# First edge layer of a two-layer graph network: GpSimd's half rows of messages in quarters, gathers in four parts

## The chip, the core and the metric

The kernel is written in Bass and Tile for one core of a Trainium2 chip. The metric is the device time of one execution in microseconds. TensorE is called PE in the profile, VectorE DVE, ScalarE ACT, GpSimd POOL, and SyncE, which issues most plain DMAs, SP. Each engine takes its own instructions in the order of the program; an instruction that has to wait for another engine, or for a DMA, holds up all that stands behind it on its engine.

## What is computed

A graph with 6,250 nodes of 512 features and 100,000 edges, sorted by their destination, goes through two layers with a layernorm and a ReLU ahead of each and a residual around each. The change is in the first one, an attention layer with 8 heads of 64 features:

```python
h = leaky_relu(feat @ W.T + b, 0.2).reshape(N, 8, 64)
e = leaky_relu(e_src[src] + e_dst[dst], 0.2)      # one logit per edge and head
m = segment_max(e, dst); ex = exp(e - m[dst]); s = segment_sum(ex, dst)
a = ex / s[dst] * dist
msg = h[src] * a[:, :, None]                      # a row of 512 per edge, scaled head by head
out = segment_sum(msg, dst)
```

The second layer takes the mean of `x[src]` over each node's edges, two products with 512 x 512 weights, and a layernorm.

## The kernel before

**Tiles and windows.** The edges are cut into four streams (`q` = 0 to 3), each stream into tiles of 128 edges. A window `k` holds three tiles (`j` = 0, 1, 2) of every stream, so 12 tiles of 128 edges; there are 66 windows. Tile (q, j) is written with two digits here, as the program does: 32 is stream 3, third tile. The streams form two pairs, `p` = 0 (streams 0 and 1) and `p` = 1 (streams 2 and 3).

**Gathers.** GpSimd fetches each tile with one indirect DMA (line 744): 128 rows of `h0_d`, 520 fp32 each (512 features and 8 source logits), chosen by the edges' source indices, into `gbuf`. This buffer has room for four windows (`NB = 4`), so the gathers that are issued in window k are those of window k + 4, and each of them overwrites a tile of window k. Before it may be issued, the matmul that reads that tile has to be done.

**Messages.** A gathered row becomes a message when each of its heads is multiplied by that edge's weight (`weigh`, line 897). VectorE does whole pairs of tiles (`message`, line 967, 128x1024, for j = 0 and 1) and the first half row of tile 02 (`message_part`, line 974). The rest of the four tiles with j = 2 is shared: ScalarE does heads one by one (`message_act`, line 986), and GpSimd does the second half, heads 4 to 7, of tile 12 and of tile 32 (`message_pool`, line 998, 128x256). These two half rows are the steps `K0` (tile 12) and `K1` (tile 32).

**Sums.** `add_up(k, p, j)` (line 1010) adds a pair's messages into the destinations' rows: two matmuls with one-hot weights, 128x64 by 128x512 fp32, the first for stream 2p, the second for 2p + 1. The steps are `A00`, `A01`, `A02` for p = 0 and `A10`, `A11`, `A12` for p = 1. The second matmul of `A02` reads tile 12, that of `A12` tile 32; so `A02` needs `K0` and `A12` needs `K1`. `finish` (lines 1027 and 1028; `C0`, `C1`) adds what the window before carries over.

**Softmax ahead.** The logits of later windows are worked on at the same time: `front_turn` and `front_copy` (transposes of the one-hot tiles, lines 806 and 810; `FT0`, `FT1`), `front_dst` (line 818; `FD`, window k + 3), `soft_src` (line 827; `SSa`, `SSb`), scans on VectorE (lines 847, 854, 861), `soft_turn` (line 873; `TE`, `TM`), `soft_back` (line 878; `CM`), `leaky` to `weigh`. `add_ones` (line 1018; `SV`) sums the softmax weights.

**The order.** Nothing is scheduled by a compiler: the list `ORDER` (line 1172) is run through once for each window and writes every engine's instructions in that order. For PE it says, from one `A12` to the next: `A12 FD SSa C1`, then in the next window `TE FT1 A00 SV A01 TM A10 A02 SSb C0 A11 FT0 A12`. For GpSimd it says `K0`, then `GA`, six gathers, then `K1`, then `GB`, six gathers. `TILES` (line 1120) gives the gathers' order: `10 01 00 30 11 20` in `GA`, and `02 22 12 21 31 32` in `GB`. What each waits for follows from the tile that it overwrites: 10 and 00 wait for `A00`; 01 and 11 for `A01`; 30 and 20 for `A10`; 02 and 12 for `A02`; 21 and 31 for `A11`; 22 and 32 for `A12`.

A gathered tile is read first by `soft_pick` (line 835): tiles with j = 0 and 1 near the end of window k + 1, tiles with j = 2 early in window k + 2.

Of the kernel before, what the change touches and what calls it, by code (L numbers as in the profile page):

```python
# [12 lines left out]
OP = mybir.AluOpType  # L13
AX = mybir.AxisListType

N, D, E, H = 6250, 512, 100000, 8
# [6 lines left out]
T = 3  # L23
# [3 lines left out]
NB = 4  # L27
# [17 lines left out]
def gnn_kernel(ctx, tc, x, srcp, dstp, attrp, wt0, b0, wsrc, wdst, wts, wtn, bias1, gamma1, beta1, out):  # L45
    nc = tc.nc
    V, A, G, S, P = nc.vector, nc.scalar, nc.gpsimd, nc.sync, nc.tensor
# [629 lines left out]
    for t in range(NT):  # L677
        if t + 3 < NT:
            norm(t + 3)
            g, i = where[t + 3]  # L680
# [42 lines left out]
    GT, ES_, OHs, OHTs, PEN, AT, ZP, E_, PB, ET, MF, MR, NX, EX, AA, WS, WC, CS, FP, FD, RS, F9, SA, AP_ = ({} for _ in range(24))  # L723
    breg = {}

    def njof(k):
        return T if k < NW - 1 else 1
# [8 lines left out]
    def gather(k, part=None):  # L736
        GT[k] = g_ = gbuf[:, k % NB]
        tiles = [(q, j) for q, j in TILES if j < njof(k)]
        if k >= NW - 3:
            tiles.sort(key=lambda t: t[1])  # L740
        n = len(tiles) // 2
        for q, j in tiles if part is None else (tiles[:n], tiles[n:])[part]:
            c = k * T + j
            G.indirect_dma_start(out=g_[:, q, j, :], out_offset=None, in_=h0_d,  # L744
                                 in_offset=bass.IndirectOffsetOnAxis(ap=idx[:, q, c:c + 1], axis=0))
# [211 lines left out]
    BK, SV, A2 = {}, {}, {}  # L957
# [33 lines left out]

        return p == 0 and first <= k < NW and k % GRP[0] and k % GRP[1]

    def message_pool(k, p):

        if njof(k) == T and not (p and k in IDLE):
            x3 = GT[k][:, 2 * p + 1, T - 1, D // 2:D].rearrange("p (h d) -> p h d", d=D // H)
            G.tensor_tensor(out=x3, in0=x3, in1=A2[k][:, T - 1, 2 * p + 1, H // 2:H].unsqueeze(2).to_broadcast([128, H // 2, D // H]),  # L998
                            op=OP.mult)

    def add_up(k, p, j):
        if j >= njof(k):
# [114 lines left out]


    TILES = [(int(t[0]), int(t[1])) for t in """
    10 01 00 30 11 20 02 22 12 21 31 32  # L1120
    """.split()]

    for q in range(NQ):
# [1 line left out]
    for k in range(NB - 1):  # L1125
        gather(k)
# [5 lines left out]
    def later(f, end=NW):  # L1132

        return lambda k, *a: f(k, *a) if 0 < k < end else None
# [18 lines left out]
    def ahead(k, part):  # L1153
        if k >= NB - 1:
            gather(k, part)
# [3 lines left out]
        FT0=(4, front_turn, 0), FT0c=(4, front_copy, 0), FT1=(3, front_turn, 1), FT1c=(3, front_copy, 1),  # L1159
        FD=(3, front_dst), ECa=(3, soft_pick, 0), SSa=(3, soft_src, 0), ECb=(2, soft_pick, 1), SSb=(2, soft_src, 1), EZ=(2, soft_copy), SCF=(2, max_before), NX=(2, max_ahead),  # L1160
        SCR=(1, max_all), TE=(1, soft_turn, 0), TM=(1, soft_turn, 1), CM=(1, soft_back), LM=(1, leaky),
        SUB=(1, soft_sub), EXP=(1, soft_exp), AA=(1, weigh),
        FL=(1, later(fac_leaky, KR)), FDf=(1, later(fac_sub, KR)), FX=(1, later(fac_exp, KR)), RS=(1, later(fac_rows, KR)),
        RH=(1, later(fac_diag, KR)), PF=(1, later(fac_spread, KR)), F9a=(1, later(fac_rest, KR)), F9b=(1, later(fac_all, KR)),
        RESC=(0, later(rescale, KR)), D0c=(0, message_part), D0a=(0, message, 0, 0), D0b=(0, message, 0, 1), D1a=(0, message, 1, 0),
        D1b=(0, message, 1, 1),
        SV=(0, add_ones), A00=(0, add_up, 0, 0), A01=(0, add_up, 0, 1), A02=(0, add_up, 0, 2),
        A10=(0, add_up, 1, 0), A11=(0, add_up, 1, 1), A12=(0, add_up, 1, 2), C0=(0, finish, 0), C1=(0, finish, 1),
        EV0=(0, evac0), EV1=(-1, evac1), OH=(4, onehot), CS=(0, later(carry_sel)),
        GA=(NB, ahead, 0), GB=(NB, ahead, 1), K0=(0, message_pool, 0), K1=(0, message_pool, 1))  # L1170
    STEPS.update({f"H{p}{i}": (0, message_act, p, i) for p in range(2) for i in range(4) if p or i})
    ORDER = """
    K0 H01 D0b S D0a D1a TE ECb H11 NX S SCR S FT1 A00 D0c FL EV1 SV S H12 RESC A01 AT0 H02 OH TM A10 GA K1 S CM FDf
    A02 FX S RS S LM RH AT0c CS SSb C0 SUB PF L FT1c S EZ EXP D1b SCF S A11 H10 AT1 ECa AT1c FT0 S AA F9a S A12 F9b S
    EV0 FD SSa C1 FT0c S GB
    """.split()

    def late_x(i):
# [384 lines left out]
    def early(w, f):  # L1563
# [3 lines left out]

    STEPS1 = dict(EV0=(0, evac1_, 0), CS0=(-1, carry_split, 0), EV1=(-1, evac1_, 1), CS1=(-1, carry_split, 1), OH=(1, onehot, 3),
                  SEL=(1, carry_sel, FR), C0=(0, finish1, 0), C1=(0, finish1, 1), G0=(3, gather1, 0), G1=(2, gather1, 1))
    STEPS1.update({f"A{p}{j}": (0, add_up1, p, j) for p in range(2) for j in range(T)})  # L1570
    SLOTS1 = dict(MEAN=(-2, slot1_mean), SUMS=(-1, slot1_sums))
    ORDER1 = """
    en en la MEAN A00 A01 A02 la A10 CS0 C0 EV1 OH en PUT en PRE G1 sl la SEL en en SUMS CS1 sl A11 A12 EV0 G0 C1 sl
    """.split()

    last, ends = none(), none()
    for k in range(-1, NW - 1):
# [5 lines left out]
        for name in ORDER1:  # L1583
# [11 lines left out]
            elif name in SLOTS1:  # L1595
                d, f = SLOTS1[name]
# [7 lines left out]
    k = NW - 1  # L1604
# [53 lines left out]
    with tc.If(fv > 0):  # L1658
# [69 lines left out]
        with tc.For_i(0, NE * 128, 128) as r:  # L1728
# [12 lines left out]
                            in0=hg[:, 0:D].rearrange("p (h d) -> p h d", h=H),  # L1741
                            in1=ga.unsqueeze(2).to_broadcast([128, H, D // H]), op=OP.mult)
# [52 lines left out]
```

## Time and profile before

| what | us |
|---|---|
| median of three runs (2717.96, 2723.20, 2725.59) | 2723.2 |
| the profiled execution, its own time | 2745.03 |
| its span, first to last instruction | 2743.2 |
| from the span's start to the first edge layer, about | 265 |
| the first edge layer, about 265 to 1455 | 1190 |
| the second layer and what follows, about | 1288 |
| GpSimd busy over the span | 1795.8 |
| PE busy over the span (weight loads apart) | 2125.4 |

A group of instructions is shown as line, engine, operation, output and inputs, shape and count, then the busy time and the mean of one in ns, then the time that the engine sat idle just before them, and what ended most of it. In the timeline each row has start, duration, engine, line and count (xN), and in brackets the idle time before it and what ended it. A releaser named "issue" means that the profile shows nothing that was waited for; ends of matmuls are modelled.

### The profile page before, as it was taken

How to read it: one execution, taken by the hardware profiler on the slowest of the kernel's cores; microseconds unless marked ns; L12 is line 12 of the kernel's file. 1: busy time of each engine (PE TensorE's matmuls, PEld its weight loads, DVE VectorE, ACT ScalarE, POOL GpSimd, SP SyncE). 2: the span in 40 equal slices, each digit the busy share in tenths (PEclk: the TensorE clock that was granted, in tenths of full speed). 3: DMA queues.
4: the chain of work that ended last, by engine and by line, in shares of the span. 5: the costliest groups of instructions: out<-in, count | busy, mean ns of one | idle time of the engine just before them, and what ended most of it. 6: DMA issues, size and time to landing. Idle time of an engine off the chain costs nothing.

```text
span 2743.2 us, 32878 instructions
## 1 busy us (share of the span) xinstructions
PE 2125.4 (77%) x8780; PEld 1052.9 (38%) x8780; DVE 1539.0 (56%) x3120; ACT 984.8 (36%) x2957; POOL 1795.8 (65%) x1803
## 2 busy tenths in 40 slices
PE   7982688888888888888884376687878788787876
PEld 5761233333333333333331133343344334343434
DVE  7874565567666766665676222354445345454545
ACT  6860344444454454444453011122222122222212
POOL 4666477777777677767762666666667666666652
PEclk9996799999999899999997588898889889898988
DMA  6636477787878878878775777777878787787872
GB/s 203 208 114 182 129 206 198 222 246 233 241 229 243 243 237 237 247 228 235 237 232 152 231 213 220 242 252 248 251 248 264 240 255 238 248 256 246 253 221 88
DMA packets 264702, 611.54 MB, mean 223 GB/s; under 512 B 63604, under 2 KB 74372, under 8 KB 264510
## 3 DMA queue, kind: packets, MB, share of 16 engines
q0 software_dynamic: 125440, 414.35, 51.7%
q1 hardware_dynamic: 138494, 193.97, 21.6%
q8 instruction: 72, 1.18, 0.2%
q10 hardware_dynamic: 576, 1.05, 0.1%
q14 instruction: 120, 0.98, 0.1%
HBM read 511.44 MB, written 97.76 MB: 222 GB/s over the span
## 4 chain that ended last, share of the span: by engine, by line
PE 31%; issue 9%; DVE 7%; another core or an unknown queue 7%; DMA 2%; ACT 1%; POOL 1%; SPq 1%; ACTq 0%; DVEq 0%; POOLq 0%
PE ps_f L592 6%; PE ps_w L1325 5%; PE ps_s L1325 5%; PE ps_b L592 5%; PE ps_w L1010 3%; PE ps_w L1333 2%; DVE gbuf L967 1%; PE ps_z L818 1%; PE ps_t L1406 1%; PE ps_w L1027 1%; PE ps_z L1406 1%; PE ps_s L1333 1%; DVE sx L1090 1%; DVE oh L787 1%
## 5 line engine op out<-in xcount | busy, mean ns | idle before, releaser
L1296 POOL DMA_INDIRECT g<-h_d,idx x784 | 774.1, 987 | 386.5 <-issue 202.5
L744 POOL DMA_INDIRECT gbuf<-h_d,idx x784 | 770.5, 983 | 348.7 <-issue 179.4
L1010 PE MATMUL ps_w<-gbuf,oh 128*64 128x512 f32 x1568 | 517.2, 663 | 94.9 <-issue 52.9
L986 ACT ACTIVATE gbuf<-gbuf,aa 128x64 f32<-128x64 f32 x1276 | 329.8, 334 | 2.3 <-DVE aa L907 0.7
L967 DVE TENSOR_TENSOR gbuf<-gbuf,ps_c 128x1024 f32<-128x1024 f32 x260 | 308.0, 1212 | 0.3 <-issue 0.3
L1325 PE MATMUL ps_s<-g,oh 128*64 128x512 f32 x784 | 193.5, 629 | 51.9 <-issue 49.2
L1325 PE MATMUL ps_w<-g,oh 128*64 128x512 f32 x784 | 217.0, 636 | 12.6 <-issue 10.6
L1010 PEld LDWEIGHTS ps_w<-gbuf,oh 128*64 128x64 f32 x1568 | 103.8, 142 | 226.7 <-issue 156.5
L1423 ACT ACTIVATE hs<-sx,slc 128x512 f32<-128x512 f32 x45 | 36.6, 813 | 419.5 <-remote 186.4
L854 DVE TENSOR_TENSOR_SCAN nx<-penb,ms,ps_z 32x256 f32<-32x256 f32 x66 | 48.1, 729 | 223.2 <-PE ps_w L1010 90.7
L1412 DVE TENSOR_TENSOR lo<-ps_t,hi 128x512 fp32r<-128x512 f32 x55 | 37.9, 688 | 229.7 <-ACT hi L1411 105.6
L628 POOL TENSOR_TENSOR pr<-hr,watt 128x1024 f32<-128x1024 f32 x47 | 113.2, 2417 | 75.5 <-DVE hr L625 70.2
L810 ACT ACTIVATE oht<-ps_t 128x384 f32<-128x384 f32 x132 | 63.7, 482 | 233.0 <-PE ps_z L818 74.3
L592 PE MATMUL ps_f<-ws_whi,hi 128*128 128x512 f32 x112 | 58.1, 519 | 106.3 <-issue 61.5
L787 DVE TENSOR_TENSOR oh<-ps_c,dsr 128x768 f32<-128x768 f32 x130 | 123.0, 947 | 1.8 <-issue 1.8
L1038 ACT ACTIVATE ws<-ps_w 128x512 f32<-128x512 f32 x103 | 60.2, 584 | 172.7 <-PE ps_w L1010 86.4
L1027 PE MATMUL ps_w<-ws,cs 128*128 128x512 f32 x170 | 99.1, 666 | 20.8 <-DVE et L885 11.3
L818 PE MATMUL ps_z<-oht,edb 128*32 128x384 f32 (+1 forms) x264 | 112.9, 557 | 1.7 <-DVE mf L847 1.7
L1325 PEld LDWEIGHTS ps_s<-g,oh 128*64 128x64 f32 x784 | 52.5, 142 | 156.8 <-issue 143.4
L806 PE MATMUL ps_t<-ident,oh 128*128 128x128 f32 x392 | 79.1, 315 | 35.8 <-issue 31.0
L998 POOL TENSOR_TENSOR gbuf<-gbuf,aa 128x256 f32<-128x256 f32 x128 | 81.3, 636 | 38.0 <-issue 18.6
L1333 PE MATMUL ps_w<-chi,cs 128*128 128x512 f32 x65 | 36.2, 557 | 80.5 <-issue 47.8
(398 smaller groups left out, 4007.5 us busy)
## 6 DMA issues: line engine op xcount, KB each, us to landing
sx<-x SPq DMA_DIRECT2D x95, 256.0 KB
acc_d<-ws SPq DMA_DIRECT2D x182, 130.2 KB
acc_d<-ws SPq DMA_DIRECT2D x182, 128.0 KB
h_d<-hr SPq DMA_DIRECT2D x49, 260.0 KB
gbuf<-h_d,idx POOLq DMA_INDIRECT x784
g<-h_d,idx POOLq DMA_INDIRECT x784
sa<-acc_d SPq DMA_DIRECT2D x48, 260.5 KB
s<-acc_d SPq DMA_DIRECT2D x48, 256.0 KB
```

Of the source, the lines that this page charges most:

```text
L592: P.matmul(pt, a_[:, k], w_[:, k], start=not last[0], stop=stop and k == 3 and w_ is whi_ and a_ is lo)
L628: G.tensor_tensor(out=pr, in0=hr[:, None, 0:D].to_broadcast([128, 2, D]), in1=watt, op=OP.mult)
L744: G.indirect_dma_start(out=g_[:, q, j, :], out_offset=None, in_=h0_d, in_offset=bass.IndirectOffsetOnAxis(ap=idx[:, q, c:c + 1], axis=0))
L787: V.tensor_tensor(out=oh.rearrange("p a j b n -> p (a j b) n"), in0=c_iota[:, None, :].to_broadcast([128, 4 * T, M]), in1=dsr[:, k].rearra ...
L818: P.matmul(z[0:NQ * H, 0:n], ed_tile(k, p), oht[:, p, 0:n], start=(p == 0), stop=False, skip_group_check=True)
L967: eng.tensor_tensor(out=x4, in0=x4, in1=(AA if eng is V else A2)[k][:, i, q].unsqueeze(3).to_broadcast([128, 2, H, D // H]), op=OP.mult)
L986: A.activation(x_, x_, AF.Copy, scale=A2[k][:, T - 1, 2 * p + q2, h:h + 1])
L1010: P.matmul(w[r, :], oh[:, p, j, q2], g_[:, 2 * p + q2, j, 0:D], start=(j == 0 and not goes_on(k, p)), stop=False, skip_group_check=True)
L1027: P.matmul(w, CS[k][:, p], c[:, p, 0:D], start=False, stop=True, skip_group_check=True)
L1296: G.indirect_dma_start(out=g_[:, q2, j, :], out_offset=None, in_=h1_d[0:NT * 128, :], in_offset=bass.IndirectOffsetOnAxis(ap=idx[:, 2 * p ...
L1325: P.matmul(BK[p][64 * q2:64 * q2 + 64, :], OHs[k][:, p, j, q2], GT[k, p][:, q2, j, :], start=(j == 0 and not goes_on(k, p, 1)), stop=False ...
L1333: P.matmul(w, CS[k][:, p], part, start=False, stop=True, skip_group_check=True)
```

## The change

The second half of a row, heads 4 to 7, is now multiplied in two instructions of two heads each, 128x128 instead of 128x256. `K0` becomes `K00` (heads 4 and 5 of tile 12) and `K01` (heads 6 and 7); `K1` becomes `K10` and `K11` for tile 32. The twelve gathers are issued in four parts of three, `G0` to `G3`, and one quarter row stands ahead of each: `K00 G0 K01 G1 K10 G2 K11 G3`. In the list of tiles, 22 moves from the eighth place to the eleventh, so the parts are `10 01 00`, `30 11 20`, `02 12 21` and `31 22 32`. The steps of the other engines keep their order.

```diff
-        n = len(tiles) // 2
-        for q, j in tiles if part is None else (tiles[:n], tiles[n:])[part]:
+        n = len(tiles) // 4
+        for q, j in tiles if part is None else tiles[n * part:n * part + n]:
...
-    def message_pool(k, p):
+    def message_pool(k, p, i):
 
         if njof(k) == T and not (p and k in IDLE):
-            x3 = GT[k][:, 2 * p + 1, T - 1, D // 2:D].rearrange("p (h d) -> p h d", d=D // H)
-            G.tensor_tensor(out=x3, in0=x3, in1=A2[k][:, T - 1, 2 * p + 1, H // 2:H].unsqueeze(2).to_broadcast([128, H // 2, D // H]),
-                            op=OP.mult)
+            h = slice(H // 2 + 2 * i, H // 2 + 2 * i + 2)
+            x3 = GT[k][:, 2 * p + 1, T - 1, h.start * 64:h.stop * 64].rearrange("p (h d) -> p h d", d=D // H)
+            G.tensor_tensor(out=x3, in0=x3, in1=A2[k][:, T - 1, 2 * p + 1, h].unsqueeze(2).to_broadcast([128, 2, D // H]), op=OP.mult)
...
-    10 01 00 30 11 20 02 22 12 21 31 32
+    10 01 00 30 11 20 02 12 21 31 22 32
...
-        EV0=(0, evac0), EV1=(-1, evac1), OH=(4, onehot), CS=(0, later(carry_sel)),
-        GA=(NB, ahead, 0), GB=(NB, ahead, 1), K0=(0, message_pool, 0), K1=(0, message_pool, 1))
+        EV0=(0, evac0), EV1=(-1, evac1), OH=(4, onehot), CS=(0, later(carry_sel)))
+    STEPS.update({f"G{i}": (NB, ahead, i) for i in range(4)})
+    STEPS.update({f"K{p}{i}": (0, message_pool, p, i) for p in range(2) for i in range(2)})
...
-    K0 H01 D0b S D0a D1a TE ECb H11 NX S SCR S FT1 A00 D0c FL EV1 SV S H12 RESC A01 AT0 H02 OH TM A10 GA K1 S CM FDf
-    A02 FX S RS S LM RH AT0c CS SSb C0 SUB PF L FT1c S EZ EXP D1b SCF S A11 H10 AT1 ECa AT1c FT0 S AA F9a S A12 F9b S
-    EV0 FD SSa C1 FT0c S GB
+    K00 H01 D0b S D0a D1a TE ECb H11 NX S SCR S FT1 A00 D0c FL EV1 SV S H12 RESC A01 AT0 H02 OH TM A10 G0 K01 G1 K10 S
+    CM FDf A02 FX S RS S LM RH AT0c CS SSb C0 SUB PF L FT1c S EZ EXP D1b SCF S A11 G2 K11 H10 AT1 ECa AT1c FT0 S AA F9a
+    S A12 F9b S EV0 FD SSa C1 FT0c S G3
```

## The prediction

> **What bounds the kernel now.** I read the page's groups, then the sums by stage, then the waits of the gathers' line, then the timelines of GpSimd and PE for a window. The chain of waits gives little here: it follows PE and VectorE through this stage and hardly meets GpSimd.
>
> ```profile
> L744 POOL DMA_INDIRECT gbuf<-h_d,idx x784 | 770.5, 983 | 348.7 <-issue 179.4
> L998 POOL TENSOR_TENSOR gbuf<-gbuf,aa 128x256 f32<-128x256 f32 x128 | 81.3, 636 | 38.0 <-issue 18.6
> 265.00:1455.00 1190.00, 994.35 (x4248) 422.70 (x4250) 786.87 (x1516) 564.32 (x2102) 823.04 (x881) 0.91 0.77 225
>   issue: 179.4, 630
>   PE ps_w L1010: 49.6, 40
>   PE ps_z L818: 35.5, 23
>   PE ps_z L827: 28.1, 25
>   PE ps_s L1018: 12.4, 9
> ```
>
> The stage takes 1190 us, in which GpSimd is busy for 823 and PE for 994. A gather takes 0.95 us and the next starts 0.30 us later (the "issue" row, 179.4 us in 630 gaps), so it costs 1.25 us; twelve are 15.0 us. A half row is 0.62 us, followed by a gap of 0.16 in place of 0.30, so it adds 0.5; two add 1.0. Over the whole stage, the idle rows named PE sum to about 126 us in 97 waits: one and a half waits in each window, of 1.3 us. GpSimd's timeline shows where they sit: ahead of 22, of 10, or of 01.
>
> ```profile
> 1029.29 0.62 POOL L998 TENSOR_TENSOR gbuf<-gbuf,aa 128x256 f32<-128x256 f32 x1
> 1030.07 0.99 POOL L744 DMA_INDIRECT gbuf<-h_d,idx  x1 [0.16 <-issue]
> 1032.62 0.94 POOL L744 DMA_INDIRECT gbuf<-h_d,idx  x1 [1.57 <-PE ps_z L818]
> ...
> 1038.26 0.95 POOL L744 DMA_INDIRECT gbuf<-h_d,idx  x1 [0.30 <-issue]
> 1039.22 0.62 POOL L998 TENSOR_TENSOR gbuf<-gbuf,aa 128x256 f32<-128x256 f32 x1
> 1040.00 0.99 POOL L744 DMA_INDIRECT gbuf<-h_d,idx  x1 [0.16 <-PE ps_w L1010]
> ```
>
> ```profile
> 1029.96 1.07 PE L1010 MATMUL ps_w<-gbuf,oh 128*64 128x512 f32 x2 [2.31 <-issue]
> 1030.96 1.48 PE L818 MATMUL ps_z<-oht,edb 128*32 128x384 f32 x4
> ...
> 1034.77 1.08 PE L1010 MATMUL ps_w<-gbuf,oh 128*64 128x512 f32 x4
> 1035.78 1.51 PE L1018 MATMUL ps_s<-ex,oh 128*128 128x18 f32 x12
> 1037.22 1.08 PE L1010 MATMUL ps_w<-gbuf,oh 128*64 128x512 f32 x4
> ```
>
> K1 ends at 1029.91 and PE, idle for 2.31 us, starts the second matmul of `A12` at 1029.96. So **K1 gates A12**, and in most windows it does. Then PE runs without a gap through FD, SSa, C1, TE, FT1 to `A00` (ends 1034.77 + 1.08 = 1035.85, 5.94 after K1) and SV to `A01` (ends 1038.30, 8.39 after K1). This closes a ring: K1, A12, A00, gather 10, five more gathers, K1. GpSimd's own way round it is longer now: from K1's end it has six gathers and K0 to do, and reaches 10 after 8.2 us at the earliest (7.41 to K0 where nothing waits, 0.62, 0.16). Sixty ends of K1 between 315.91 and 1398.95 make 59 windows of **18.36 us**, 16.0 us of work, about 1.9 of waits for PE and 0.45 of gathers that take over 0.95.
>
> How late PE's word can be is shown by the waits themselves:
>
> ```profile
> 747.70 0.98 POOL L744 DMA_INDIRECT gbuf<-h_d,idx  x1 [1.78 <-PE ps_s L1018]
> 1096.50 0.94 POOL L744 DMA_INDIRECT gbuf<-h_d,idx  x1 [1.24 <-PE ps_z L827]
> ```
>
> The first is gather 10, 9.83 us after the end of K1 (737.87); the second is 01, 11.64 after it (1084.86), though the records draw `A01` as over by 1093.27. Such waits are seldom between 0.3 and 1 us: GpSimd goes on about 1.1 us or more after its last gather ended, even where the matmul is drawn as done before that. So I treat PE's drawn ends as a floor, not as the moment of release.
>
> **The change, part by part.**
>
> *Quarter rows.* Two 128x256 go, four 128x128 come, 4 a window for 62 windows. No 128x128 multiply of GpSimd is in this trace. Its rows of 128x256 (0.62 to 0.64 us) and 128x512 (1.23 to 1.28) give 2.4 ns an element with next to nothing fixed: 0.31. The nearest smaller one, 128x195 on line 382, takes 0.54. I take 0.33, nearer to the proportional end as the operation is the same. Each then adds 0.33 + 0.02 + 0.16 - 0.30 = 0.21, four 0.84, against 1.0 now: -0.2 us a window, +0.7 at the other bound. [...]
>
> *K11's place, the part that decides.* A12 now needs K11, which stands behind nine gathers, with three behind it. From its end GpSimd does 31, 22, 32 (0.16 + 0.99 + 0.30 + 0.95 + 0.30 + 0.95 = 3.65 us) and K00 (0.35), and stands at 10 after 4.2 us, or 5.4 where 22 waits as it does now. PE needs 5.94 at least for `A00` and 8.39 for `A01`. So gathers 10 and 01 wait in every window, and K01, G1, K10, G2 and K11 stand behind 01. That queue from the start of 01 to the end of K11:
> - 01 and 00: 0.95 + 0.30 + 0.95 = 2.20
> - K01: 0.02 + 0.33, then a gap of 0.16: 0.51
> - G1: 0.99 + 0.30 + 0.95 + 0.30 + 0.95 = 3.49; K10 0.51; G2 3.49; K11 0.35
>
> in all 10.55, and 0.30 more since a gather's mean is 983 ns and not 946 (8 x 37). The window is then the start of 01 after K11, plus 10.85. The start of 01 has three prices: 8.39 + 0.30 = 8.7 (drawn end, no delay); 11.7 (the usual start of 01 where it waits today, as 11.64 above); and what I take, **9.6**: GpSimd is at rest after 10, and its release comes some 1.1 us after that rest began, or 0.9 after `A01`. I lean to the low side since GpSimd now rests for 4 to 5 us a window just there. That makes 20.45.
>
> *K01's place.* `A02` needs K01, which now stands behind G0; it ends at 9.6 + 2.55 = 12.2 after K11, while PE is at `A02` after about 10. PE's queue behind it (SSb, C0, A11, FT0) comes some 2 us later, and so do ScalarE's copy for SSb and VectorE's scan after it. The cover is PE's wait for K11 at 20.45: A11 is through by about 15.5, and 21, which waits for it, is issued at about 18.9. That costs nothing while the cover of 3 us holds. The same holds for 30 (`A10`, 2 us of cover) and 02 (`A02`, 3 us). With PE's word late by 1 to 4 us as above, each of the three will sometimes wait; I put one wait of 1.3 us in every third window: 0.45. Bounds: none, or one in every window.
>
> *22 to the eleventh place.* Its wait of 1.3 us for `A12` stays, as again one gather lies between K11 and it, but is hidden in the rest ahead of 10. The tiles land later by up to three gathers (4 us); their first reader is most of a window away (line 835). No SP queue is passed, and no DMA is added.
>
> *The sum.* 20.45 + 0.45 = 20.9 against 18.36: +2.54 a window. 61 windows run from one full set of gathers to the next: +155 us on the profiled 2745.0. Scaled to the median, 2723.2 / 2745.0 x 155 = 154: **2877**. The mechanism's own bounds are 19.55 (+73: 2795, without delays) and 22.55 (+256, so 2977, with 01 as late as where it waits today), plus 1.3 if every window waits once more.
>
> [...]
>
> **The rivals.**
>
> *The gathers flow and 22's wait goes* (faster). If PE's `A00` and `A01` were out 4 and 5.5 us after K11, GpSimd would not rest ahead of 10 and 01, and 22's wait, 0.85 a window on average in the idle column, could go: 61 x 0.85 = 52 us, **2671**. For it: PE idles 2.31 us ahead of `A12`. Against: PE has 5.94 and 8.39 us of matmuls in its fixed order; the point where this wins is 7.5 us for the start of 01 (18.36 - 10.85), below the drawn end.
>
> *PE's word comes as late as today.* 01 starts at 11.7 after K11: 22.55, with further waits hidden: +4.2 x 61 = 256, **2977**. For it: the row at 1096.50. Against: PE has less to do in that time, and GpSimd rests.
>
> *PE's word comes at once.* 01 at 8.7, no further wait: 19.55, +73, **2795**. For it: the scan on VectorE that waits for SSa (line 854) often starts within 0.1 us of its drawn end. Against: the waits that cluster above 1 us.
>
> *The order does not bite*: K11 may be let through early and A12 be held by VectorE or ScalarE instead, as in windows where PE's gap is 0. Then the loss is a few us, no change. In the trace A12 starts 0.05 after K1 in most windows, so this is faint.
>
> **How the numbers follow.** Chances: my forecast, 20 to 22 us a window, 0.52; late word 0.23; word at once 0.18; faster rival 0.04; order does not bite 0.03. About 0.3%, 8 us, is what a measurement of this kernel tells from no change. Slower 0.93, same 0.03, faster 0.04. The range leaves out the two last and the outer half of the late case: 2785 to 2965.
>
> **What would show it.** Right: gathers 10 and 01 idle by 1 us and more in nearly every window of the changed kernel; windows of 20 to 22 us; PE's idle time ahead of A12 growing from about 1 to 4 us and more; line 1000's 128x128 at 0.31 to 0.36 us; the second layer unchanged near 1288 us. Wrong: 01 waiting no more than now, or windows below 18.4 us; A02's wait for K01 growing until A11 is what K11 waits for would show that I priced the wrong gate.

## The result, and the profile after

| | median us | runs |
|---|---|---|
| before | 2722.57 | 2717.96 to 2725.59 (4) |
| after | 2920.64 | 2914.28 to 2925.28 (4) |
| ratio | 1.0732 | 95% interval 1.0705 to 1.0759 |

The change makes the kernel 198 us slower; 154 were forecast. The profiled execution of after took 2914.3 us, 169.3 more than the one of before. The other 29 us are the two profiles' distance from their medians: that of before ran 22 above its median, that of after 6 below.

First the groups of after, with the columns as before: busy time, mean of one, idle time ahead and what ended most of it. Then what ended the idle time ahead of the gathers, summed over the first layer, with the number of waits.

```profile
L744 POOL DMA_INDIRECT gbuf<-h_d,idx x784 | 758.9, 968 | 516.6 <-PE ps_w L1010 291.5
...
L1010 PE MATMUL ps_w<-gbuf,oh 128*64 128x512 f32 x1568 | 582.1, 647 | 252.9 <-issue 133.3
...
L999 POOL TENSOR_TENSOR gbuf<-gbuf,aa 128x128 f32<-128x128 f32 x256 | 104.5, 409 | 39.0 <-DVE slc L198 18.5
```

```profile
  PE ps_w L1010: 291.5, 107
  issue: 169.3, 642
```

The gathers' idle time grew from 348.7 to 516.6 us, and of the 347 us that are not issue, 291.5 have one name now: `add_up`'s matmuls, in 107 waits, so 2.7 us a wait. In before, four lines of PE shared some 126 us. PE's own idle time ahead of line 1010 grew too, from 94.9 to 252.9. Each engine waits for the other: the ring that the prediction drew. A quarter row takes 0.41 us, where 0.33 was taken.

GpSimd's timeline for one window of after (start, duration, in brackets the idle time ahead):

```profile
1024.50 0.99 POOL L744 DMA_INDIRECT gbuf<-h_d,idx  x1 [0.16 <-issue]
1025.79 0.95 POOL L744 DMA_INDIRECT gbuf<-h_d,idx  x1 [0.30 <-issue]
1027.05 0.95 POOL L744 DMA_INDIRECT gbuf<-h_d,idx  x1 [0.30 <-issue]
1028.02 0.41 POOL L999 TENSOR_TENSOR gbuf<-gbuf,aa 128x128 f32<-128x128 f32 x1
1032.03 1.12 POOL L744 DMA_INDIRECT gbuf<-h_d,idx  x1 [3.60 <-PE ps_w L1010]
1034.43 0.94 POOL L744 DMA_INDIRECT gbuf<-h_d,idx  x1 [1.29 <-DVE s_v L185]
1035.68 0.95 POOL L744 DMA_INDIRECT gbuf<-h_d,idx  x1 [0.30 <-issue]
1036.65 0.41 POOL L999 TENSOR_TENSOR gbuf<-gbuf,aa 128x128 f32<-128x128 f32 x1
...
1044.80 0.41 POOL L999 TENSOR_TENSOR gbuf<-gbuf,aa 128x128 f32<-128x128 f32 x1
```

K11 has ended at 1024.34. Gathers 31, 22 and 32 and the quarter row K00 follow without a wait, 22 too. Then GpSimd rests 3.60 us ahead of 10 and 1.29 ahead of 01, and from there everything flows until the next K11 (the last row). The name "DVE s_v" beside the second rest is a releaser that happened to come last in the records; the drawn end of `A01` is 0.26 us earlier, as the next view shows. Over the layer the gaps ahead of 10 and of 01 have means of 3.97 and 1.36 us; all the others are 0.16 or 0.3. A window takes 21.31 us, against 18.36 in the profile of before.

The same stretch on PE:

```profile
1024.40 1.97 PE L1010 MATMUL ps_w<-gbuf,oh 128*64 128x512 f32 x2 [3.93 <-issue]
1026.29 2.01 PE L818 MATMUL ps_z<-oht,edb 128*32 128x384 f32 x4
...
1030.64 1.08 PE L1010 MATMUL ps_w<-gbuf,oh 128*64 128x512 f32 x4
1031.64 1.51 PE L1018 MATMUL ps_s<-ex,oh 128*128 128x18 f32 x12
1033.09 1.08 PE L1010 MATMUL ps_w<-gbuf,oh 128*64 128x512 f32 x4
...
1037.11 1.07 PE L1010 MATMUL ps_w<-gbuf,oh 128*64 128x512 f32 x2 [0.78 <-issue]
...
1045.26 1.97 PE L1010 MATMUL ps_w<-gbuf,oh 128*64 128x512 f32 x2 [3.07 <-issue]
```

PE rests 3.93 us, then does the second matmul of `A12`. **That matmul takes 1.97 us; in before the same one took 1.07.** FD behind it takes 2.01 in place of 1.48, and so `A01` ends at 1034.17, 9.83 after K11, not 8.39. The sums by stretch say why; the columns are busy time of PE, its weight loads, VectorE, ScalarE and GpSimd, then PE's granted clock, the DMA share and GB/s.

```profile
265.00:1617.00 1352.00, 1073.23 (x4144) 427.95 (x4145) 764.03 (x1471) 555.93 (x2060) 832.53 (x1006) 0.89 0.70 196
1024.00:1027.40 3.40, 3.00 (x4) 0.65 (x5) 0.00 (x0) 0.00 (x0) 2.63 (x4) 0.50 0.89 264
1027.40:1044.90 17.50, 14.01 (x63) 6.04 (x61) 12.85 (x26) 8.84 (x33) 10.70 (x14) 0.99 0.80 236
```

The granted clock is **0.50 for the 3.4 us around PE's restart** and 0.99 for the rest of the window. The stage takes 1352 us, 162 more than the 1190 before; what follows takes 1295, 7 more than before.

### The profile page after: what moved, and what is told of

Its sections match the earlier page's. It is cut to its first block, busy times and chain, and to the rows that moved or that the text cites. A ratio compares the mean times of both kernels' runs of the same rounds, so it can differ in the third digit from the quotient of the medians.

```text
span 2912.4 us, 33065 instructions
## 1 busy us (share of the span) xinstructions
PE 2223.7 (76%) x8780; PEld 1068.5 (37%) x8780; DVE 1536.5 (53%) x3120; ACT 987.1 (34%) x2957; POOL 1803.3 (62%) x1931
## 3 DMA queue, kind: packets, MB, share of 16 engines
q1 hardware_dynamic: 138494, 193.97, 20.9%
## 4 chain that ended last, share of the span: by engine, by line
PE 43%; issue 21%; DVE 11%; POOL 11%; another core or an unknown queue 7%; ACT 3%; DMA 3%; SPq 1%; ACTq 0%; POOLq 0%; DVEq 0%
POOL gbuf L744 9%; PE ps_w L1010 7%; PE ps_b L592 6%; PE ps_w L1326 5%; PE ps_s L1326 5%; PE ps_f L592 5%; PE ps_z L818 3%; PE ps_w L592 1%; PE ps_w L1027 1%; PE ps_w L1334 1%; POOL gbuf L999 1%; DVE gbuf L967 1%; PE ps_z L827 1%; PE ps_t L1407 1%
## 5 line engine op out<-in xcount | busy, mean ns | idle before, releaser
L744 POOL DMA_INDIRECT gbuf<-h_d,idx x784 | 758.9, 968 | 516.6 <-PE ps_w L1010 291.5
L1010 PE MATMUL ps_w<-gbuf,oh 128*64 128x512 f32 x1568 | 582.1, 647 | 252.9 <-issue 133.3
L1038 ACT ACTIVATE ws<-ps_w 128x512 f32<-128x512 f32 x103 | 60.6, 588 | 406.6 <-PE ps_w L1027 393.1
L818 PE MATMUL ps_z<-oht,edb 128*32 128x384 f32 (+1 forms) x264 | 158.8, 748 | 5.5 <-DVE mf L847 5.5
L847 DVE TENSOR_TENSOR_SCAN mf<-penb,mf,ps_z 32x384 f32<-32x384 f32 (+1 forms) x65 | 64.5, 993 | 131.3 <-issue 106.7
L999 POOL TENSOR_TENSOR gbuf<-gbuf,aa 128x128 f32<-128x128 f32 x256 | 104.5, 409 | 39.0 <-DVE slc L198 18.5
L1346 ACT ACTIVATE ws<-ps_w 128x512 f32<-128x512 f32 x66 | 39.3, 596 | 177.9 <-remote 79.0
```

The lines of the kernel that those rows point to most:

```text
L818: P.matmul(z[0:NQ * H, 0:n], ed_tile(k, p), oht[:, p, 0:n], start=(p == 0), stop=False, skip_group_check=True)
L1010: P.matmul(w[r, :], oh[:, p, j, q2], g_[:, 2 * p + q2, j, 0:D], start=(j == 0 and not goes_on(k, p)), stop=False, skip_group_check=True)
```

## The experiments

The runs fell on several chips, and the kernel before does not take the same time on all of them: 2487 us where e1 to e4 ran, 2721 us for after_again, before_again, e5 and e6, and 2487 us again for the last four. Ratios are taken within one chip only. `after` itself ran only where before takes 2721 us or so, twice; e1 to e4 never ran there, so they are compared with each other and by their windows. A window's mean is taken over some 56 windows in the middle of the first layer.

**e1, the split alone.** The kernel before, with each half row done as two quarters back to back in its old place.

```diff
-    K0 H01 ... A10 GA K1 S CM FDf
+    K00 K01 H01 ... A10 GA K10 K11 S CM FDf
```

> The kernel before with each half row cut into two quarters that stand back to back in the old places; gathers in two parts and in the old order, as before. Theory (the loss is K11's place): the split alone costs the quarters' own time, four of 0.41 us (measured in the changed kernel) for two of 0.62, about 0.2 us for each pair beyond the half row: 61 x 0.44 = 27 us, so about 2750. Rival (short instructions on GpSimd are what costs): most of the 198 us, 2850 or more.

Measured: 2496.37 against 2487.53, ratio 1.0032 (1.0017 to 1.0046). Splitting costs some 9 us, a third of the 27 expected. The loss is in the places.

**e2, the places alone.** The kernel after with whole half rows at K01's and K11's places: K0 behind G0, K1 behind G2.

```diff
-    K00 H01 ... A10 G0 K01 G1 K10 S
+    H01 ... A10 G0 K0 G1 S
...
-    ... A11 G2 K11 H10 ...
+    ... A11 G2 K1 H10 ...
```

> The changed kernel, but each half row whole again (128x256), K0 at K01's place behind G0 and K1 at K11's place behind G2. Theory: the ring from K1 over A12, A00 and A01 to gathers 10 and 01 and back is as long as in the changed kernel, 10.3 + 10.9 = 21.2 us a window, so about 2915. Rival (short instructions): half or more of the loss goes, 2820 or less.

Measured: 2759.79, ratio 1.1093 (1.106 to 1.1125). Its groups:

```profile
L744 POOL DMA_INDIRECT gbuf<-h_d,idx x784 | 754.7, 963 | 547.9 <-PE ps_w L1010 367.7
...
L1010 PE MATMUL ps_w<-gbuf,oh 128*64 128x512 f32 x1568 | 585.0, 651 | 262.8 <-POOL gbuf L998 241.2
```

The same picture as after, with whole half rows: gathers wait for line 1010, line 1010 for the half row. Here the profile names it outright (241.2 us). Windows of 21.46 us, gaps of 4.45 ahead of 10 and 1.42 ahead of 01.

**e3, K11 back.** The kernel after with K11 beside K10, ahead of G2 in place of behind it; K01 stays late.

```diff
-    ... A10 G0 K01 G1 K10 S
+    ... A10 G0 K01 G1 K10 K11 S
-    ... A11 G2 K11 H10 ...
+    ... A11 G2 H10 ...
```

> The changed kernel with K11 moved ahead of G2, beside K10; all else stays, K01 behind G0 too. Theory: six gathers again lie between the last quarter of tile 32 and gather 10, the ring is open, PE's idle time ahead of A12 falls below 1.5 us, the window comes back to 18.4 to 19 us: 2730 to 2770. Rival (K01's place, A02's wait, carries much of the loss): 2830 or more.

Measured: 2485.08, ratio 0.9997 (0.9982 to 1.0012). Only one quarter row stands elsewhere than in after, three gathers earlier, and **the whole loss is gone**; e2, with the late place, took 275 us more on the same chip. Windows are 16.87 us long, and PE rests 0.14 us ahead of `A12` on average; its rest has moved to `A02`, and few gathers wait for it:

```profile
L744 POOL DMA_INDIRECT gbuf<-h_d,idx x784 | 771.5, 984 | 226.4 <-issue 127.5 <-PE ps_w L1010 22.6 <-PE ps_t L806 15.5
L1010 PE MATMUL ps_w<-gbuf,oh 128*64 128x512 f32 x1568 | 520.0, 627 | 117.7 <-POOL gbuf L999 114.9 <-ACT ws L1042 1.7 <-DVE gbuf L967 1.0
```

**e4, PE kept at work.** The kernel after, with FT0's three transposes, which stand ahead of `A12`, done five times over (the same values each time). PE then rests less while K11 is awaited, at the price of more work.

```diff
-        for j in range(njof(k)):
-            P.transpose(...)
+        for _ in range(1 if p else 5):
+            for j in range(njof(k)):
+                P.transpose(...)
```

> The changed kernel with the three transposes of FT0 done five times over into the same bank with the same result, which fills some 2.2 us of PE's idle time ahead of A12. Theory (PE's rest of 3 to 4 us ahead of A12 halves its clock for the first 3.4 us after it, and A01 is out after 10.2 us in place of 8.4): the granted clock stays at 1.0 there, 01 starts 8.7 us after K11, the window falls from 21.3 to about 19.5 us, 2920 to about 2810, though PE does more. Rival (the clock is no cause, or PE is short of time): 2920 or more.

Measured: 2676.17, ratio 1.0755 (1.0726 to 1.0783). `after` was not on this chip; e2, the nearest to it, took 2759.79. So with **12 more transposes in each window the kernel is 84 us quicker** than that. Its windows are 20.1 us long, not the 19.5 expected: the 15 transposes take 1.86 us where three take 0.55, so some 1.3 us of the rest are filled and not 2.2, and PE still rests 2.0 us ahead of `A12` on average. The run was repeated later as e4_again, where PE's timeline and clock show both cases side by side (lines are one higher in this kernel):

```profile
1015.59 1.07 PE L1011 MATMUL ps_w<-gbuf,oh 128*64 128x512 f32 x2
1018.43 1.07 PE L1011 MATMUL ps_w<-gbuf,oh 128*64 128x512 f32 x2 [1.76 <-POOL gbuf L1000]
1019.43 1.48 PE L819 MATMUL ps_z<-oht,edb 128*32 128x384 f32 x4
...
1037.86 1.27 PE L1011 MATMUL ps_w<-gbuf,oh 128*64 128x512 f32 x2 [2.62 <-DMA h_d<-sx]
1039.06 2.77 PE L819 MATMUL ps_z<-oht,edb 128*32 128x384 f32 x4
```

```profile
1018.40:1021.80 3.40, 3.37 (x11) 1.28 (x12) 0.42 (x1) 0.51 (x3) 2.66 (x3) 1.00 0.84 277
1037.90:1041.30 3.40, 3.40 (x6) 0.86 (x7) 0.00 (x0) 0.00 (x0) 2.73 (x3) 0.60 0.84 238
```

Both rests end with K11 (the second one's K11 ends at 1037.81, though the record names a DMA). After a rest of 1.76 us the clock stays at 1.00 and FD takes 1.48; after one of 2.62 the clock is 0.60 over the next 3.4 us and FD takes 2.77. Sorted by whether half clock follows K11 at all, the windows of the three kernels fall into two kinds:

| kernel | full clock: windows, 01 after K11, window | half clock: windows, 01 after K11, window |
|---|---|---|
| after | 2, 8.66, 19.48 | 54, 10.59, 21.38 |
| e2 | 4, 8.66, 19.60 | 52, 10.71, 21.61 |
| e4_again | 35, 8.68, 19.49 | 21, 10.28, 21.07 |

In 40 of the 54 windows of after half clock was recorded for 3.4 us, and 01 starts 10.27 us after K11; in 14 it was recorded for 6.8 us, and 01 starts at 11.51.

**before and after again.** Both once more on one chip, before with a second profile.

> The changed kernel once more, beside the experiments. Theory: as the late half rows (21.46 us a window and 1.109 of before on a chip where before took 2487.5 us), within 1%: 1.10 to 1.12 there, 1.073 where before takes 2722 us. Rival (the quarters cost something of their own): 2% or more above the late half rows.

> The kernel before once more, for its profile. Theory: where it takes about 2490 us, its windows are 16.9 us and gathers 22, 10 and 01 start 0.3 us after the drawn end of the matmul they wait for; where it takes about 2720, the windows are 18.3 us and PE's word comes 1 to 4 us after the drawn end.

Measured: after 2923.55 against 2721.22, ratio 1.0741 (1.0723 to 1.0759), windows of 21.37; before 2718.06 in one execution, windows of 18.05. The result stands, and the window of before is 18.05 where the execution is as quick as the median, not the 18.36 of the profile that the prediction was made from.

**e5, K01 back.** The kernel after with K01 beside K00 at the head of the window; K11 stays late.

```diff
-    K00 H01 ... A10 G0 K01 G1 K10 S
+    K00 K01 H01 ... A10 G0 G1 K10 S
```

> The changed kernel with K01 moved back to the head of the window, beside K00; K11 stays behind G2. Theory: K01's place is free, so nothing comes back but a gap of 0.2 us: a window of 21.1 to 21.5 us, within 1.5% of the changed kernel. Rival (A02's wait for K01 carries part of the loss): 3% or more below the changed kernel.

Measured: 2901.72, ratio 1.0666 (1.065 to 1.0681), 22 us less than after_again on that chip. Windows of 21.05 to 21.07, some 0.30 less. PE no longer waits at `A02`, but rests longer ahead of `A12`: 4.90 us in place of 3.36. So `A02`'s wait was covered, and the 0.30 came from GpSimd: K01 left the queue between 01 and K11, where it cost 0.02 + 0.41, with a gap of 0.16 behind it in place of 0.30: 0.29 us.

**e6, K1 early.** The kernel before with K1 whole, behind three gathers and not six.

```diff
-    K0 H01 ... A10 GA K1 S CM FDf
+    K0 H01 ... A10 G0 K1 G1 S CM FDf
...
-    EV0 FD SSa C1 FT0c S GB
+    EV0 FD SSa C1 FT0c S G2 G3
```

> The kernel before, half rows whole, tiles in the old order, but K1 stands behind the first three gathers of the window instead of behind six (K0 G0 K1 G1 G2 G3). Theory: nine gathers lie between K1 and gather 10, A12 no longer waits for K1 but for ScalarE or VectorE, PE's rest and the waits ahead of 22, 10 and 01 shrink: 0.3 to 0.8 us a window less, 1 to 2% faster than before. Rival (K1 no longer sets anything once six gathers follow it): the same as before within 0.3%.

Measured: 2721.53, ratio 0.9998 (0.9986 to 1.001), windows of 18.13. PE's rest ahead of `A12` falls to 0.1 us or less and nothing is gained: the idle time ahead of the gathers only changes its names. Lines 1010, 818 and 827 and the releaser "remote" had 41.2, 38.1, 26.6 and 8.8 us of it in before_again, and have 50.8, 7.5, 12.8 and 31.8 here.

**e7, the tiles' order alone.** The kernel before with 22 in the eleventh place.

```diff
-    10 01 00 30 11 20 02 22 12 21 31 32
+    10 01 00 30 11 20 02 12 21 31 22 32
```

> The kernel before with the changed order of the tiles alone: 22 in the eleventh place, half rows and parts as before. Theory: 22's wait for A12 (0.85 us a window in before) is taken over by 10 or 01, which stand two gathers behind it and wait for PE anyway: no change, ratio 0.995 to 1.003, windows within 0.3 us of those of before. Rival: the wait ahead of 22 is a cost of its own and goes: 0.85 x 61 = 52 us, ratio 0.98 on a chip whose kernel before takes 2720 us.

Measured: 2488.85 against 2487.10, ratio 1.0004 (0.9992 to 1.0016), windows of 17.01. As expected; but here, where before takes 2487 us, the gathers wait little in any case (249.6 us idle ahead of line 744, 80 waits for line 1010 of 0.49 on average, against 348.7 and 40 of 1.24 in the first profile of before), and where it takes 2721 the rival was not tried.

**e3 and e4 again**, the same two kernels.

> The changed kernel with K11 beside K10, ahead of G2, once more. On a chip whose kernel before took 2487 us this tied with it (ratio 0.9997). Theory: K11's late place, with PE's rest and its lowered clock, is all of the loss; four quarters at 0.41 us with their gaps cost 0.3 to 0.4 us a window more than two half rows at 0.64, so the ratio lies between 0.998 and 1.008 on any chip, PE idles under 0.5 us ahead of A12, and no half-clock stretch follows K11. Rival: on a chip whose kernel before takes 2720 us, where GpSimd is released late after PE's matmuls, an early K11 takes away waits as well: ratio 0.98 to 0.99. The windows' mean tells them apart: 17.8 to 18.5 against under 17.6 us, where that of before is 18.1 to 18.4.

> The changed kernel with FT0's transposes made five times over (the same values each time), so that PE is at work while it would wait for K11. Theory: what the window lost beyond the drawn ring is PE's clock, at 0.5 for 3.4 us after each rest; with the rest filled, 01 starts 8.7 to 9.3 us after K11 in place of 10.5, windows of 19.5 to 20.1 in place of 21.3, and the ratio is 1.04 to 1.05 on a chip where the changed kernel gives 1.073. Rival: the loss is the queue of GpSimd alone; then more work on PE can only cost: ratio 1.07 or above, windows of 21.3 or more. On a chip whose kernel before takes 2487 us, 1.0755 as in the first run.

Measured: e3_again 2487.87, ratio 1.0002 (0.9993 to 1.0012), windows of 16.98; e4_again 2680.04, ratio 1.0762 (1.0743 to 1.0782). Both repeat their first runs. What e3 would give where before takes 2721 us stays open.

**e8, both half rows first.** The kernel before with K0 K1 at the head of the window and then twelve gathers.

```diff
-    K0 H01 ... A10 GA K1 S CM FDf
+    K0 K1 H01 ... A10 GA S CM FDf
```

> The kernel before with both half rows, whole, at the head of the window, K0 K1, and then the twelve gathers in GA and GB. Theory: once K1 is early, A12 is held by other engines and the window by GpSimd's own work (two half rows and twelve gathers, 16.0 us, and what waits are left for PE's word): PE idles under 0.5 us ahead of A12, ratio 0.985 to 1.003. If the window of before is set by PE's release of gathers alone, the waits move to other places and nothing is gained (ratio 0.997 to 1.003); if K1's place costs anything in before, this shows it, as a ratio under 0.995. Rival: K1 at the head waits itself for the weights of tile 32, which VectorE makes ready late, and holds up twelve gathers: ratio above 1.005, with an idle row named DVE ahead of K1.

Measured: 2470.44, ratio **0.9934** (0.9922 to 0.9947). It is the only kernel clearly quicker than before on its chip, by 0.7%; after did not run there. The gathers' group and GpSimd's timeline:

```profile
L744 POOL DMA_INDIRECT gbuf<-h_d,idx x784 | 781.2, 996 | 239.3 <-issue 151.8
```

```profile
1002.77 0.94 POOL L744 DMA_INDIRECT gbuf<-h_d,idx  x1 [0.30 <-issue]
1004.02 0.94 POOL L744 DMA_INDIRECT gbuf<-h_d,idx  x1 [0.30 <-issue]
1004.97 1.19 POOL L998 TENSOR_TENSOR gbuf<-gbuf,aa 128x256 f32<-128x256 f32 x2
1006.32 0.99 POOL L744 DMA_INDIRECT gbuf<-h_d,idx  x1 [0.16 <-issue]
```

No gather waits beyond the 0.3 us between two issues; windows of 16.69 us, 0.32 less than e7's. GpSimd's own work sets the pace. PE's rest moved from `A12`, where it is 0 now, to `A02`, which waits for K0 (0.67 us in this window, 3.21 in the next), and no gather is late for it. Whether e8 gains where before takes 2721 us was not tried; e6, with K1 nearly as early, gained nothing there.

## Why the prediction was right, and where it was off

**K11's place: right.** K11 gates `A12`, GpSimd stands at 10 after 4.1 us (4.2 predicted), rests ahead of 10 and 01 in nearly every window, and the queue from 01 to K11 sets the rest. PE's rest ahead of `A12` grew from 0.79 to 3.36 us on average ("from about 1 to 4 us and more", so somewhat less than foreseen). e3 undoes this place alone and the loss is gone; e2 makes this place without the split and the loss is there.

**The start of 01: the step that failed.** The prediction took 9.6 us after K11, as 8.39 for the drawn end of `A01`, 0.3, and a release "some 1.1 us after that rest began, or 0.9 after `A01`". The runs showed another thing. 01 starts 10.52 after K11 on average, and only 0.3 us after `A01`'s drawn end: PE's word is not late in this kernel. `A01` itself is late, by 1.84 us on average (10.23 in place of 8.39), because PE was granted half its clock (0.50) after its rest, for 3.4 us in 40 of the 56 windows and for 6.8 in 14. The prediction has no term for PE's clock. The 8.7 that the prediction kept as the lower price is right to 0.04 us in the windows without half clock, but those are 2 of 56. The number 9.6 was near for a wrong reason.

How long PE's rests were, and how often half clock followed, is counted here over all rests above 0.5 us between 300 and 1300 us of the eleven traces of after, e1 to e5, e7, e8 and the repeats of after, e3 and e4. The traces of before, before_again and e6 are not in the table; there half clock follows shorter rests too, as the last section says.

| PE's rest, us | rests | share followed by half clock within 6 us |
|---|---|---|
| 0.5 to 1.5 | 319 | 0 |
| 1.5 to 2 | 96 | 0.09 |
| 2 to 2.5 | 67 | 0.42 |
| 2.5 to 3 | 94 | 0.79 |
| 3 to 3.5 | 90 | 0.88 |
| over 3.5 | 105 | 1.00 |

So in these traces half clock followed 42% of the 67 rests of 2 to 2.5 us and each of the 105 over 3.5. The prediction foresaw a rest of 4 us for PE and did not weigh what might follow it.

**The queue from 01 to K11: nearly right.** 10.85 predicted, 10.79 measured. Two errors cancel: three quarter rows at 0.41 and not 0.33 add 0.24, and the 0.30 for stretched gathers was not there.

**The further waits: wrong, small.** 0.45 a window was put down for waits at 30, 02 or 21; their gaps are 0.16 or 0.3 us. In the sum: 20.9 + 0.92 (start of 01) - 0.06 (queue) - 0.45 = 21.31, as measured.

**The quarter rows: mis-sized.** 0.41 lies between the bounds of 0.31 and 0.54, nearer to the former. Halving the row took 0.62 to 0.41, not to 0.31. In their four places the quarters then cost 4 x (0.41 + 0.02 + 0.16 - 0.30) = 1.16, 0.16 a window more than the two half rows, some 10 us in all; no run measures this alone. In e1 they stand in pairs and keep GpSimd busy for 108.8 us, where e7's half rows take 80.7: 28 us more. But its gathers are 12 us less busy than e7's, and GpSimd idles 9 us less ahead of them, so only some 7 are left; the whole kernel lost 9. So in e1, where nothing but the cut was made, there was no gain.

**K01's place and 22: right.** `A02` did wait for K01 (0.78 us ahead of 1037.11, where K01 has ended at 1037.06), and PE's rest ahead of `A12` covered it, as e5 shows. 22's wait is gone into the rest ahead of 10.

**What the loss is made of**, against the 18.05 us of before's second profile: 1.43 a window, 87 us, for the ring at full clock (19.48), and 1.83, some 112 us, for the clock; in all 199 over 61 windows. At full clock the time would have been some 2722.6 + 87 = 2810, worked out and not measured in one run; e4, where half clock follows K11 in 21 of 56 windows instead of 52, went that way. The window of before, 18.36 in a profile that ran above its median, hid 0.31 a window, 19 us of the 44 by which the forecast fell short; the other 25 are the 0.41 a window between 20.9 and 21.31.

**The rivals.** "The order does not bite" and "the gathers flow" are refuted by the rows above. "PE's word comes at once" is what happened, and its ring of 19.55 us is the full-clock window of 19.48; only its clock was missing. "PE's word comes as late as today" gave a time on the far side (2977); its start of 01 at 11.7 was not seen as a mean.

## What to carry to other kernels

Where two engines shared a ring here, the small piece of work that gates the other had to stand early in its engine's queue: e3, with K11 three gathers earlier than in after, took 2485 us, and e2, with the late place, 2760 on the same chip. Look at what is behind such a piece (here three gathers) and ahead (nine). Cutting a producer in pieces gained nothing here (e1: ratio 1.0032), where the first piece lets nobody go on, since the matmul of `A12` reads the whole row. And before giving PE a rest in every period, look in the trace for what it costs to start again at half clock: in after, with rests of 3.36 us on average ahead of `A12`, 1.8 us of every window, more than half of the loss.

## What the runs showed of the hardware

The same program, the kernel before, took 2721 us on some chips and 2487 on others, with repeats within 0.5% on each, the first profiled execution (2745) apart. The experiments went to three chips, each at one time, so a chip is not told apart from its hour. Kernels with a late K11 differ little there: windows of 21.31 and 21.37 us for after where before takes 2721, 21.46 for e2 where it takes 2487, and 19.5 at full clock on both. Where the gathers stream they differ: the first layer of before took 1190 us on the one, that of e7, which ties with before, some 1065 on the other. What follows the first layer differs as much, 1288 against 1158 us.

On the chips of 2721 us, in before, gathers go on late after PE's drawn ends: where 01 waited in before_again, it started 3.1 us after the drawn end of `A01` (median of 25 waits), against 0.27 in e7. VectorE's scan on line 854 is late in part of the windows only: half of its 44 waits in before_again ended within 0.11 us of line 827's drawn end, a quarter 5 us or more after it. And half clock follows a rest of 0.5 to 1 us nearly as often as not (46% of 154, in before, before_again and e6), where in the table it never does. In after, where before takes as long, releases come within 0.3 us, and half clock follows none of the 84 rests of 0.5 to 1 us in after, after_again and e5. No run shows why the two kernels differ in this, and it stays open.
